# Paged attention after three conditional layers: a batch's fourth value gather is issued behind a GpSimd copy of a number that VectorE makes

## The chip, the cores and the metric

The kernel runs on one core of a Trainium2 chip, in fp32. The metric is the time of one execution in microseconds (us) of the device. The core's engines are TensorE (PE in the profile; its weight loads are PEld), VectorE (DVE), ScalarE (ACT), GpSimd (POOL) and SyncE (SP). Each engine works through its own queue of instructions in order and waits on semaphores that other engines or finished DMAs raise.

## The reference

Four residual layers on `x` of 32 batches x 32 positions x 512 channels. The first three are matrix products whose weights are picked by batch; the change does not touch them. The fourth is attention with a paged cache, and its inner part is what the change lies in:

```python
x = x + token_mixing(x); x = x + lora_linear(x); x = x + adapter_linear(x)
q = rope(rmsnorm(x @ Wq.T)); k = rope(rmsnorm(x @ Wk.T)); v = x @ Wv.T    # 32 query heads, 8 key heads, d = 128
kc = k_cache[block_table]                   # 16 pages of 32 positions: 512 cached keys a batch
vc = v_cache[block_table]                   # and 512 cached values
k_all = concat([kc, k]); v_all = concat([vc, v])                           # 544 positions
scores = where(valid, q @ k_all.T / sqrt(d), -1e30)                        # valid: cached position < cache_seqlens
x = x + (softmax(scores) @ v_all) @ Wo.T
```

## The kernel before, in words

The span has four parts: the three linear layers (to about 180 us), the projections to queries, keys and values (to about 375 us), the attention loop (to about 1086 us) and an end in which the last output projections are left over. The change lies in the attention loop alone.

**Units.** The loop runs over units (b, g): 32 batches b, and in each batch 8 key heads g, so 256 units, with a tail of 8 more steps. A unit has 128 rows: 4 query heads that share a key head, times 32 positions. Step n = 8b + g of the loop does the following, for several units at once. The order of the instructions on every engine is the order in which the program writes them (`manual_schedule`); semaphores are set by what tiles are read and written.

1. DMAs are issued: on SP's queue the key pages, queries and new values of the coming batch, and on GpSimd's queue, for batches from 2 on, one of the four gathers of cached values of the batch (`load_value_chunk`, L252: an indirect DMA of 128 rows of the cache, each row 8 heads x 128 numbers, into the tile `vt`). Gather c is issued at the step of g = c, for c = 0 to 3. The gathers of batches 0 and 1 are issued before the loop. The two batches in flight have a home pool each.
2. `scores(b, g)`: TensorE makes 288 and then 256 scores a row (L1023, L1024) in one PSUM tile `s_ps`, which has a single buffer. VectorE then does one `tensor_tensor_reduce` (L1032): it scales the scores, masks them, writes the result `pr` to SBUF, and the row's minimum to the tile `low` of 128 x 1, which has four buffers. The scores of the next unit can be written to `s_ps` only when this has read them.
3. `exponentials(b, g)`: ScalarE takes the exponential of `pr` with `low` as its bias and sums the row (L1048).
4. `flip_kept` (L1160): an earlier batch's outputs are transposed by VectorE for the output projection.
5. `place(b, q, j)` for the quad (four units) that ended before: VectorE transposes a quarter of the quad's exponentials in blocks of 32 x 32 (L1061, into `turned`, two buffers); four copies bring it into `placed`, which are shared out by a pattern: in the steps of the second quad's place two by ScalarE (L1075) and two by VectorE (L1079), in the last of these three and one, and in those of the first quad two each by ScalarE and GpSimd (L1077), or one and three in the first batches. For quad q = 0 of batch b this runs at the steps g = 4 to 7 of batch b, for q = 1 at the steps g = 0 to 3 of batch b + 1. At j = 0 GpSimd copies the columns of the new keys to `pq` (L1086), and at j = 2 TensorE transposes them (L1090, into `pn_ps`).
6. `share`: 0, 1 or 2 matmuls of the output projection (L1180, into `f_ps`) of four batches that are done. Their numbers follow a pattern of 32 steps, so four batches in a row differ and the fifth is like the first.
7. `values` for the unit 8 steps back: one product for each of the four gathers of that batch, `placed` with `vt` (L1103, into `o_ps`); with the fourth unit the new values (L1123) and the division by the sums on VectorE (L1137, L1139).

The gather and the loop's order around it read:

```python
                if g < L // P and b >= 2:
                    load_value_chunk(b, g)
                ...
                scored = scores(b, g)
                exponentials(*scored)
```

with L // P = 4. What `scores` returns ends with the tile `low` of its unit.

Of the kernel before, what the change touches and what calls it, by code (L numbers as in the profile page):

```python
# [12 lines left out]
F32 = mybir.dt.float32  # L13
# [7 lines left out]
P = 128  # L21
# [4 lines left out]
L = NPP * PSIZE  # L26
# [33 lines left out]
def cond_resid_kernel(  # L60
# [18 lines left out]
    nc = tc.nc  # L79
    H2 = D // 2  # L80

    const = ctx.enter_context(tc.tile_pool(name="const", bufs=1))
# [86 lines left out]
    def load_table(b: int):  # L169

        pages_of[b] = const.tile([1, NPP], I32, tag="pages", name=f"pages_{b}", bufs=4)
        at = B + b * NPP
        nc.sync.dma_start(out=pages_of[b], in_=pick[:, at : at + NPP])
# [34 lines left out]
    def load_keys(b: int):  # L208

        pool = homes[b % 2]  # L210
        kt = pool.tile([P, NPP + 1, HK * PSIZE], F32, tag="kt", name=f"kt_{b}")
        kts[b] = kt
# [9 lines left out]
    def load_new_keys(b: int):  # L222
        nc.sync.dma_start(out=kts[b][:, NPP, :], in_=k_d[b])

    def load_queries(b: int, q: int):

        qts[b, q] = qp.tile([P, HALF * S], F32, tag="qt", name=f"qt_{b}_{q}")
        nc.sync.dma_start(
            out=qts[b, q], in_=q_d[b][:, q * HALF * S : (q + 1) * HALF * S]
        )  # L230

    def load_inverses(b: int):
        rqs[b] = const.tile([P, 2, QUAD], F32, tag="rq", name=f"rq_{b}", bufs=2)
        nc.sync.dma_start(out=rqs[b], in_=r_d[:, b * S : (b + 1) * S])

    def page_keys(b: int):
        return [kts[b][:, n, :] for n in range(NPP)]
# [10 lines left out]
    def load_value_chunk(b: int, c: int):  # L248
        if c == 0:
            vts[b] = homes[b % 2].tile([P, L // P, HK * D], F32, tag="vt", name=f"vt_{b}")  # L250
        at = b * (L // P) + c
        nc.gpsimd.indirect_dma_start(  # L252
            out=vts[b][:, c, :],
            out_offset=None,
            in_=v_cache,
            in_offset=bass.IndirectOffsetOnAxis(ap=v_idx[:, at : at + 1], axis=0),
        )

    def load_new_values(b: int):

        vn = vnp.tile([P, HK // QUAD, D], F32, tag="vn", name=f"vn_{b}")
        vns[b] = vn
        for u in range(QUAD):
            nc.sync.dma_start(
                out=vn[u * S : (u + 1) * S, :, :],
                in_=v_d[b * S : (b + 1) * S, :].rearrange("s (q u d) -> u s q d", u=QUAD, d=D)[u],
            )
# [57 lines left out]
    def store_values(vs, c: int, t: int, eng):  # L325
        c0 = (c - (HQ + HK) // REP) * HID
        eng.dma_start(out=v_d[t * P : (t + 1) * P, c0 : c0 + HID], in_=vs)
# [589 lines left out]
    def load_wo(h: int):  # L917
        i, h0 = (0, h) if h < HQ - LATE else (1, h - (HQ - LATE))
        nc.sync.dma_start(out=wos[i][:, h0 : h0 + 2, :], in_=o_d[:, h : h + 2, :])
# [93 lines left out]
    def quad_of(b: int, g: int):  # L1013
        return b, g // QUAD

    def scores(b: int, g: int):
        kt, qt = kts[b], qts[quad_of(b, g)]
        kt4 = kt.rearrange("d n (h o) -> d n h o", h=HK)

        ps = ps_s.tile([P, 2 * L], F32, tag="s", name=f"s_ps_{b}_{g}")  # L1020
        u = g % QUAD
        q = qt[:, u * REP * S : (u + 1) * REP * S]
        nc.tensor.matmul(ps[:, first:L], q, kt4[:, :N_LOW, g, :], start=True, stop=True)  # L1023
        nc.tensor.matmul(  # L1024
            ps[:, L : first + LT], q, kt4[:, N_LOW:, g, :], start=True, stop=True
        )
        if u == 0:
            prs[quad_of(b, g)] = tp.tile([P, QUAD, LT], F32, tag="pr", name=f"pr_{b}_{g}")
        pr = prs[quad_of(b, g)][:, u, :]
        low = tp.tile([P, 1], F32, tag="low", name=f"low_{b}_{g}", bufs=4)  # L1030

        nc.vector.tensor_tensor_reduce(  # L1032
            pr,
            ps[:, first : first + LT],
            mask,
            rqs[b][:, g // QUAD, u : u + 1],
            3.0e38,
            ALU.add,
            ALU.min,
            low,  # L1040
        )
        return b, g, pr, low

    def exponentials(b: int, g: int, pr, low):
        quad, u = quad_of(b, g), g % QUAD
        if u == 0:
            dens[quad] = tp.tile([P, QUAD], F32, tag="den", name=f"den_{b}_{g}", bufs=4)
        nc.scalar.activation(  # L1048
            pr, pr, AF.Exp, bias=low, scale=-1.0, accum_out=dens[quad][:, u : u + 1]
        )  # L1050
# [99 lines left out]
    def flip_kept(n: int):  # L1150

        while kept and kept[0][3] <= n:
            b, q, o, _ = kept.pop(0)
            t, j = divmod(b, BT)
            if (t, q) not in ots:
                i = (2 * t + q) % 3
                ots[t, q] = places[i].tile(
                    [P, HALF, P], F32, tag=f"ot_{i}", name=f"ot_{t}_{q}", bufs=1
                )
            nc.vector.transpose(  # L1160
                ots[t, q][:, :, j * S : (j + 1) * S],
                o.rearrange("p (k d) -> p k d", d=S),
            )
# [3 lines left out]
    def load_residual(t: int):  # L1167
        x3s[t] = tp.tile([P, HID], F32, tag="os", name=f"x3_{t}")
        nc.sync.dma_start(out=x3s[t], in_=x_d[t])
# [83 lines left out]
    with tc.manual_schedule(engines=order):  # L1253
        for n in range(N + LAG):
            b, g = divmod(n, HK)
            if n == FILLED + 2:
                pa.close()
                late = ctx.enter_context(tc.tile_pool(name="b_w", bufs=1))
                places.append(late)
                wos[1] = late.tile([P, LATE, HID], F32, name="wo_1")  # L1260
            if BEGIN <= n <= N and n % (BT * HK) == 0:

                load_residual((n - BEGIN) // (BT * HK))
            if n < N:
                if g == 0 and b >= 1:
                    load_queries(b, 1)
                if g == 0 and 1 <= b < B - 1:
                    load_keys(b + 1)
                    load_new_keys(b + 1)
                    keys.dsts = page_keys(b + 1)  # L1270
                    keys.transfer(slice(0, 12))
                if g < L // P and b >= 2:
                    load_value_chunk(b, g)
                if g == QUAD and b < B - 1:
                    load_queries(b + 1, 0)
                    load_inverses(b + 1)
                    if b >= 1:
                        keys.transfer(slice(12, NPP))
                    if 1 <= b < B - 2:
                        load_table(b + 2)  # L1280
                if g == QUAD + 1 and b >= 1:
                    load_new_values(b)
                if g == QUAD + 2 and b < B - 2:
                    keys = Picked(nc.sync, k_cache, pages_of.pop(b + 2), range(NPP), K_SHAPE)
                scored = scores(b, g)
                exponentials(*scored)
            flip_kept(n)
            anew = n >= LAG and not filled
            if not anew:
                fill(n)  # L1290
            if n in unstored:
                store_values(*unstored.pop(n))
            if n == QUAD + 1:
                load_new_values(0)
            if n in WO_AT:
                load_wo(2 * WO_AT.index(n))
            if QUAD <= n < N + QUAD:
                bq, i = divmod(n - QUAD, HK)
                q, j = divmod(i, QUAD)
                if j == 0:  # L1300
                    gather_new(bq, q)
                if j == 2:
                    flip_new(bq, q)
                place(bq, q, j)
            begins = (n - BEGIN) % (BT * HK) == 0
            if not begins:
                share(n)
            if n >= LAG:
                values(*units[n - LAG])
            if anew:  # L1310
                fill(n)
            if begins:
                share(n)
            if n < N and g == HK - 1 and b < B - 1:
                see_keys(b + 1)
            if n > N + QUAD:
                at = 4 * (n - N - QUAD - 1)
                finish(NT - 1, range(at, at + 4))
        assert not dens and not prs and not pos and not placed and not pns
        load_residual(NT - 1)  # L1320
        flip_kept(N + LAG)
        finish(NT - 1, range(3 * QUAD, HALF))
        finish_by_halves(NT - 1)
# [76 lines left out]
```

## Time and profile before

| What | Value |
|---|---|
| median of 3 runs | 1136.5 us (1135.73 to 1137.75) |
| the profiled execution's own time | 1136.3 us |
| its span, first to last instruction | 1134.5 us |
| granted TensorE clock | 1.0 |
| PE busy, whole span | 1119.1 us, 99% |
| PE busy in the attention loop, 375 to 1086 us | 703.6 of 711 us |
| VectorE, ScalarE, GpSimd busy in the loop | 562.8, 539.4, 302.9 us |
| the gathers L252 on GpSimd, all | 128 times, 0.95 us each (median) |
| a gather from its issue to its landing | 4.5 / 7.7 / 9.9 us (least, median, most) |
| the reduction L1032 on VectorE | 256 times, 0.78 us each |

How to read it: the span is the time from the first to the last instruction of one profiled execution, and 1.8 us of that execution lie outside it. "Busy" is time in which the engine has an instruction under way. In the timeline a line is: start in us from the span's start, busy us, engine, source line, operation, the tile written, an arrow, and the tiles read, shapes, and how many instructions of this kind the row takes together. A square bracket at its end gives the idle time before it and what is held to have ended it.

### The profile page before, as it was taken

The numbers are of one execution on the slowest core, as the hardware profiler recorded it, in microseconds if no ns is written. First come the engines' busy times: TensorE is split into PE (matmuls) and PEld (weight loads), VectorE is DVE, ScalarE is ACT, GpSimd is POOL, SyncE is SP. The second block draws the span as 40 slices with busy tenths as digits, with TensorE's granted clock in tenths as the row PEclk, the third lists the DMA queues.
The fourth block names the chain that finished last, engine by engine and source line by source line (L and its number), as shares of the span: only waits on it lengthen the run. The fifth ranks groups of instructions, "written<-read, shape, count | busy, mean of one in ns | idle before, by whom it ended". The sixth has DMA issues, their size and how long they took to land.

```text
span 1134.5 us, 19093 instructions
## 1 busy us (share of the span) xinstructions
PE 1119.1 (99%) x5480; PEld 738.0 (65%) x5480; DVE 812.3 (72%) x1674; ACT 739.3 (65%) x1885; POOL 561.0 (49%) x730
## 2 busy tenths in 40 slices
PE   8999999999999899999999999999999999999998
PEld 5554444444444688777777777777777777777766
DVE  2510688887877578878778878887877787877861
ACT  1211377676666677678877777777777877777850
POOL 3411689899798455543444344334433443344410
PEclk9999999999999999999999999999999999999999
DMA  8998447688886687778767756775777676766600
GB/s 319 391 419 352 177 130 211 162 246 221 210 234 176 203 267 264 254 255 301 241 210 243 260 190 212 264 244 183 234 239 240 199 234 223 253 201 212 231 28 10
DMA packets 173355, 259.24 MB, mean 229 GB/s; under 512 B 31522, under 2 KB 130466, under 8 KB 168770
## 3 DMA queue, kind: packets, MB, share of 16 engines
q1 hardware_dynamic: 152226, 184.22, 51.4%
q0 software_dynamic: 20016, 71.97, 17.8%
q10 hardware_dynamic: 1008, 1.84, 0.4%
q8 instruction: 44, 0.72, 0.3%
q14 instruction: 61, 0.50, 0.1%
HBM read 228.46 MB, written 37.88 MB: 235 GB/s over the span
## 4 chain that ended last, share of the span: by engine, by line
PE 61%; DVE 2%; ACT 0%; issue 0%; DVEq 0%
PE o_ps L1103 19%; PE f_ps L1180 18%; PE s_ps L1023 11%; PE s_ps L1024 9%; PE o_ps L1123 2%; PE pn_ps L1090 1%; PE f_ps L1200 1%; PE f_ps_last L1200 1%; DVE placed L1079 1%; PE qkv L312 1%; DVE pr L1032 0%; DVE turned L1061 0%; ACT placed L1075 0%; DVE os L1139 0%; DVE ot L1160 0%
## 5 line engine op out<-in xcount | busy, mean ns | idle before, releaser
L1075 ACT COPY placed<-turned 32x512 f32<-32x512 f32 x524 | 322.6, 616 | 30.2 <-DVE turned L1061 24.2
L1103 PEld LDWEIGHTS o_ps<-vt,placed 128*128 128x128 f32 x2048 | 264.2, 191 | 110.9 <-issue 74.6
L1032 DVE CUSTOM_DVE_ANT_0 pr<-s_ps,mask,rq 128x544 f32<-128x544 f32 x256 | 200.4, 783 | 129.6 <-PE s_ps L1024 106.4
L1048 ACT ACTIVATE pr<-pr,low 128x544 f32<-128x544 f32 x256 | 191.6, 748 | 142.6 <-DVE low L1032 116.1
L1077 POOL COPY placed<-turned 32x512 f32<-32x512 f32 x279 | 169.6, 608 | 222.2 <-DVE turned L1061 173.5
L1103 PE MATMUL o_ps<-vt,placed 128*128 128x128 f32 x2048 | 272.0, 276 | 3.9 <-DVE os L1139 3.3
L1180 PE MATMUL f_ps<-wo,ot 128*128 128x512 f32 x480 | 240.6, 593 | 0.0
L1061 DVE STREAM_TRANSPOSE turned<-pr 128x512 f32<-128x512 f32 x256 | 178.6, 698 | 0.1
L1023 PE MATMUL s_ps<-kt,qt 128*128 128x288 f32 x512 | 174.0, 421 | 4.2 <-DVE low L1032 2.4
L1024 PE MATMUL s_ps<-kt,qt 128*128 128x256 f32 x512 | 152.3, 379 | 0.0
L252 POOL DMA_INDIRECT vt<-in_v_cache_dram,v_idx x128 | 124.3, 971 | 36.6 <-issue 25.7
L1024 PEld LDWEIGHTS s_ps<-kt,qt 128*128 128x128 f32 x512 | 97.3, 190 | 26.8
L438 POOL TENSOR_TENSOR ra<-ra,rs 128x512 f32<-128x512 f32 x80 | 103.8, 1303 | 10.7 <-DVE rs L433 8.1
L1079 DVE COPY placed<-turned 32x512 f32<-32x512 f32 x221 | 101.9, 461 | 5.6
L1180 PEld LDWEIGHTS f_ps<-wo,ot 128*128 128x128 f32 x480 | 86.9, 190 | 25.1 <-issue 13.9
L1086 POOL COPY pq<-pr 128x128 f32<-128x128 f32 x64 | 18.5, 288 | 151.6 <-ACT pr L1048 111.2
L1023 PEld LDWEIGHTS s_ps<-kt,qt 128*128 128x128 f32 x512 | 78.2, 191 | 17.3 <-DVE low L1032 6.1
L451 ACT ACTIVATE sq<-x 128x128 f32<-128x128 f32 x256 | 76.2, 301 | 19.8 <-DVE x L409 13.6
L548 ACT COPY r<-m 128x512 f32<-128x512 f32 x80 | 46.3, 579 | 52.4 <-PE m L393 50.4
L393 PE MATMUL m<-t_pair,x_sums 128*128 128x512 f32 x160 | 75.4, 594 | 0.7 <-ACT r L548 0.7
L393 PE MATMUL m<-w_pair,x3t 128*128 128x512 f32 x160 | 75.2, 592 | 0.0
L393 PE MATMUL m<-w_pair,x_sums 128*128 128x512 f32 x160 | 72.1, 593 | 0.0
(129 smaller groups left out, 1231.8 us busy)
## 6 DMA issues: line engine op xcount, KB each, us to landing
kt<-in_k_cache_dram SPq DMA_DIRECT2D x512, 128.0 KB
wa<-in_w_adapt_dram SPq DMA_DIRECT2D x32, 1024.0 KB
q_d<-st SPq DMA_DIRECT2D x128, 128.0 KB
qt<-q_d SPq DMA_DIRECT2D x64, 256.0 KB
w_pair<-in_w_qkv_dram SPq DMA_DIRECT2D x20, 512.0 KB
o_d<-in_w_o_dram SPq DMA_DIRECT2D x16, 512.0 KB
wo<-o_d SPq DMA_DIRECT2D x16, 512.0 KB
k_d<-st SPq DMA_DIRECT2D x32, 128.0 KB
```

Of the source, the lines that this page charges most:

```text
L252: nc.gpsimd.indirect_dma_start(out=vts[b][:, c, :], out_offset=None, in_=v_cache, in_offset=bass.IndirectOffsetOnAxis(ap=v_idx[:, at : at ...
L393: nc.tensor.matmul(ps, of[:, k], by[:, k], start=(not more and k == 0), stop=(k == KH - 1), skip_group_check=more,)
L1023: nc.tensor.matmul(ps[:, first:L], q, kt4[:, :N_LOW, g, :], start=True, stop=True)
L1024: nc.tensor.matmul(ps[:, L : first + LT], q, kt4[:, N_LOW:, g, :], start=True, stop=True)
L1032: nc.vector.tensor_tensor_reduce(pr, ps[:, first : first + LT], mask, rqs[b][:, g // QUAD, u : u + 1], 3.0e38, ALU.add, ALU.min, low,)
L1048: nc.scalar.activation(pr, pr, AF.Exp, bias=low, scale=-1.0, accum_out=dens[quad][:, u : u + 1])
L1061: nc.vector.transpose(part, pr)
L1075: nc.scalar.copy(dst, src)
L1077: nc.gpsimd.tensor_copy(dst, src)
L1079: nc.vector.tensor_copy(dst, src)
L1103: nc.tensor.matmul(po, pt[:, c, :], vt[:, c, g * D : (g + 1) * D], start=(c == 0 and q == 0), stop=(c == L // P - 1 and q == 1),)
L1180: nc.tensor.matmul(pfs[t][:, :HID], ots[t, h // HALF][:, h % HALF, :], wo(h), start=(h == 0), stop=(h == (HQ if t < NT - 1 else HALF) - 1),)
```

## The change

The fourth gather (c = 3) of batches 2 to 31 is no longer issued at the head of the step g = 3. It is issued at the step g = 2, behind the instructions of `scores`, and ahead of it GpSimd copies one number, the first row of the `low` that VectorE's reduction of unit g = 2 has just made, to a tile `seen` that nothing reads. As GpSimd's queue is in order, the gather comes behind that copy, and the copy waits for the reduction. The first three gathers stay where they are, and in the order of GpSimd's queue the fourth passes no other instruction.

```diff
     def quad_of(b: int, g: int):
         return b, g // QUAD
 
+    seen = const.tile([1, 1], F32, name="seen")
+
+    def see_reduced(low):
+        nc.gpsimd.tensor_copy(seen, low[:1, :])
+
     def scores(b: int, g: int):
 ...
-                if g < L // P and b >= 2:
+                if g < 3 and b >= 2:
                     load_value_chunk(b, g)
 ...
                 scored = scores(b, g)
+                if g == 2 and b >= 2:
+                    see_reduced(scored[-1])
+                    load_value_chunk(b, 3)
                 exponentials(*scored)
```

On the other engines' queues the instructions and their order are the same. One wait is new there: the tile `low` of unit 2 gets its buffer back with unit 6, so VectorE's reduction of unit 6 now waits for GpSimd's copy too. The instruction takes that wait itself and a separate semaphore instruction ahead of it takes the one for TensorE.

## The prediction

> **What bounds the kernel now.** I read the page, then the waits, then the timeline of single batches. From the page (head, and the first line of its chain):
>
> ```profile
> span 1134.5 us, 19093 instructions
> ...
> PE 1119.1 (99%) x5480; PEld 738.0 (65%) x5480; DVE 812.3 (72%) x1674; ACT 739.3 (65%) x1885; POOL 561.0 (49%) x730
> ...
> PEclk9999999999999999999999999999999999999999
> ...
> PE 61%; DVE 2%; ACT 0%; issue 0%; DVEq 0%
> ```
>
> TensorE is busy throughout at full clock. Freeing GpSimd, VectorE or the DMAs gains nothing by itself; what can be won or lost is the little time in which a matmul waits. I number a batch's units 0 to 7, call "step" the time from a unit's first score matmul (L1023) to the next unit's, and "reduction" L1032. The view of waits, VectorE:
>
> ```profile
> DVE pr L1032 <- PE s_ps L1024: 106.4, 110, 4.5
> ...
> DVE pr L1032 <- PE pn_ps L1090: 14.8, 24, 0.7
> ```
>
> (Columns: total us, count, longest.) The second line is odd: 24 reductions sit up to 0.7 us, put down to a small transposition that they don't read. The timeline shows where, here batch 18 from unit 2 on (start, length, engine):
>
> ```profile
> 779.43 0.94 POOL L252 DMA_INDIRECT vt<-in_v_cache_dram,v_idx  x1 [0.30 <-issue]
> 779.59 1.02 DVE L1079 COPY placed<-turned 32x512 f32<-32x512 f32 x2
> ...
> 779.83 0.59 PE L1024 MATMUL s_ps<-kt,qt 128*128 128x256 f32 x2
> ...
> 781.23 0.78 DVE L1032 CUSTOM_DVE_ANT_0 pr<-s_ps,mask,rq 128x544 f32<-128x544 f32 x1 [0.62 <-PE pn_ps L1090]
> ...
> 782.12 0.71 PE L1023 MATMUL s_ps<-kt,qt 128*128 128x288 f32 x2
> ...
> 785.60 0.75 PE L1023 MATMUL s_ps<-kt,qt 128*128 128x288 f32 x2
> ...
> 787.53 0.97 PEld L1103 LDWEIGHTS o_ps<-vt,placed 128*128 128x128 f32 x8 [0.72 <-ACT placed L1075]
> ...
> 788.52 0.65 PE L1023 MATMUL s_ps<-kt,qt 128*128 128x288 f32 x2
> ```
>
> Unit 2's scores end at 780.42, VectorE's copies at 780.61, yet the reduction starts at 781.23. I read this place in batches 2 to 31. In 24 of them (all but 2, 8, 17, 21, 22, 31) it starts 0.78 to 0.92 us after the **end of the fourth gather** (here 780.37), whether the scores ended 0.19 before that end (batches 3, 4), 0.06 after, or 0.35 after (5, 9, 13, 25, 29). The delay follows the gather, not the scores; by what mechanism the profile does not say. I call it the hold. Behind the first three gathers, each followed at once by other GpSimd work, it does not show (unit 1's reduction starts 0.27 us after the third, as soon as VectorE is free).
>
> Batch 22 tries the change out: its first gather came 2.2 us late, so the fourth began after unit 2's reduction had ended (871.98).
>
> ```profile
> 870.52 0.59 PE L1024 MATMUL s_ps<-kt,qt 128*128 128x256 f32 x2
> ...
> 871.19 0.78 DVE L1032 CUSTOM_DVE_ANT_0 pr<-s_ps,mask,rq 128x544 f32<-128x544 f32 x1
> ...
> 872.28 0.94 POOL L252 DMA_INDIRECT vt<-in_v_cache_dram,v_idx  x1 [0.30 <-issue]
> ...
> 872.64 0.85 DVE L1079 COPY placed<-turned 32x512 f32<-32x512 f32 x2
> ...
> 873.93 0.78 DVE L1032 CUSTOM_DVE_ANT_0 pr<-s_ps,mask,rq 128x544 f32<-128x544 f32 x1 [0.44 <-PE s_ps L1024]
> ```
>
> There the reduction begins 0.08 us after its scores, step 3 is 3.418 us (batch 18: 785.60 - 782.12 = 3.47) and step 4 is 2.770 (batch 18: 788.52 - 785.60 = 2.93).
>
> **The change part by part.**
>
> *The fourth gather leaves the hold's place.* On GpSimd it passes nothing: ahead of it only the copy is put in, and the copy waits for unit 2's reduction. What the hold costs TensorE differs by batch, because four batches make a period of the output projection. Batches 5, 9, ... 29 all take 23.280 us from unit 0 to the next batch's, held or not: slack covers it there. In the 18 batches 6, 7, 10, 11, 12, 14, 15, 16, 18, 19, 20, 23, 24, 26, 27, 28, 30, 31, step 3 is 3.42 to 3.52 and step 4 2.93: the late reduction makes the next scores late, then VectorE's transposition and ScalarE's last placed copy, for which the o_ps matmuls wait (the L1103 line above). Bringing each to 3.418 and 2.770 (batch 22; batch 8 has 3.418 and 2.771) saves 1.30 us over the 18 in step 3 and 18 x 0.159 = 2.86 in step 4. In batches 3 and 4, steps 2 and 3 are 3.017 + 2.662 and 3.116 + 2.661, where the unheld batch 2 has 2.354 + 2.560: 0.77 + 0.86 = 1.63. Together **-5.8 us**.
>
> *A wait at unit 6.* The tiles `low` have four buffers, so unit 6's reduction overwrites what GpSimd's copy reads of unit 2. GpSimd did so 11 us before, but the instruction order shows that this reduction now carries a second wait: one semaphore instruction that waits for TensorE, then the reduction with a wait for GpSimd. Unit 4's reduction has that form already. Batch 8, unit 4, then unit 6:
>
> ```profile
> 558.13 0.59 PE L1024 MATMUL s_ps<-kt,qt 128*128 128x256 f32 x2
> ...
> 558.88 0.78 DVE L1032 CUSTOM_DVE_ANT_0 pr<-s_ps,mask,rq 128x544 f32<-128x544 f32 x1 [0.18 <-PE s_ps L1024]
> ...
> 563.47 0.59 PE L1024 MATMUL s_ps<-kt,qt 128*128 128x256 f32 x2
> ...
> 564.11 0.78 DVE L1032 CUSTOM_DVE_ANT_0 pr<-s_ps,mask,rq 128x544 f32<-128x544 f32 x1 [1.25 <-PE s_ps L1024]
> ```
>
> With VectorE idle, unit 4 starts 147 ns after its scores' end, unit 6 only 38. So 0.109 us more (0 to 0.15 as ends; I take the same form's own row). In batches 5, 9, ... and 4, 8, ... unit 7's scores come 0.87 us after that reduction: hidden. In the 16 batches b mod 4 = 2 or 3 (steps of 1.97 us) they start 0.06 us after it, in lock step: 16 x 0.109 = **+1.74 us**.
>
> *GpSimd's copy and its wait.* Queued behind the waiting copy are the fourth gather and the copy L1086, which waits for ScalarE's exponentials 3 us later anyway. No row has a copy of one number; the nearest are a 128x1 memset (0.10 to 0.12 us) and L1086 (128x128, 0.288); I take 0.2, as nearer the middle. With 0.06 from VectorE to GpSimd and 0.16 from a GpSimd copy to a gather, the gather starts some 0.41 us after the reduction's end (0.32 to 0.51), 2 to 3 us later than before. Its landing is 7.7 us (median), and its first matmul reader comes 14 us after the issue. GpSimd's first placed copies of a batch (unit 4's step) come after the landings, now with 0.14 to 2.45 us to spare, so they may be up to 1 us late; GpSimd then works 1.26 us of a step of 2.7 and catches up: **0**. Uncovered it would be at most 1 us a batch.
>
> *The gather beside VectorE's copies.* They start 0.67 and 1.10 us after the reduction, 0.26 and 0.68 into the gather. Before, a copy L1079 that started 0.16 to 0.52 into a gather ran 0.414 to 0.419 us as always, one at 0.57 to 0.60 took 0.58 to 0.62, one at 0.69 took 0.50, one past 0.79 took 0.42. So about +0.08 a batch (0 to 0.2). Unit 3's reduction waits for TensorE 0.30 to 0.48 us in batches without the hold, which hides it: **0**. Without that cover it would be 18 x 0.08 = 1.5 us.
>
> Sum: -5.8 + 1.74 = **-4.05 us**. The profiled execution took 1136.3 (span 1134.5 and 1.8 around it), so 1132.25; the median of the runs shown, 1136.5, is 0.2 above it: **1132.5**. Ends: nothing paid at unit 6, 1130.7; unit 6 at 0.15 and a quarter of the holds left, 1134.6.
>
> **The rivals.**
>
> *The hold moves with the gather* (no change). Unit 3's scores will end about 0.6 us after the moved gather's end. If a hold until 0.78 to 0.92 follows there, that reduction starts 0.15 to 0.28 late, as it is in held batches now (0.30 after the scores instead of 0.04), and step 4 stays at 2.93. Then 2.86 us of the gain are lost: -1.2, **1135.3**. For: the hold did catch scores that ended 0.35 after the gather. Against: in batches 22 and 2 scores ended 0.68 and 0.71 after the fourth gather and were not held. These are just two, and 6 of 30 batches weren't held at all.
>
> *The gather blocks VectorE's copies.* If a running gather kept out both copies until its end (0.41 + 0.95 = 1.36 after the reduction), two of 0.42 would end at 2.20, and unit 3's reduction at 2.24 would be 0.29 later than TensorE allows (batch 22: 873.93 - 871.98 = 1.95). Price as before: **1135.3**. Against: in batch 18 the copies start 0.16 into the gather and both end 0.24 after it, where a blocked pair would need 0.84. The Trainium skill, "SBUF — State Buffer", section "Who interferes with whom", has this rule: VectorE and GpSimd share a port pair as an exclusive lock, and whichever starts first fully blocks the other. The trace agrees only for a copy that starts late in the gather, and then by 0.2 us at most.
>
> *The hold isn't the gather's* (slower). If it hung on unit 2 itself (its transposition L1090, ScalarE's exponentials or the landing of keys), moving the gather would leave it, and only costs remain: +1.74 at unit 6, and, as a held batch has no slack in step 4, the 1.5 of the slowed copies: **1139.7** (1138.2 if they are not slowed). It decides if unit 2's reduction still starts over 0.7 us after its scores with no gather ended near it. For: the profile names L1090, and no mechanism ties VectorE to an issued gather. Against: the spread of 0.54 us in the scores' ends that leaves the start fixed to the gather's, and batch 22.
>
> That the gather is not moved at all is excluded by GpSimd's order.
>
> **How the numbers follow.** Forecast 0.55, hold moves 0.20, blocked copies 0.05, hold stays 0.20. A measurement of this kernel tells about 0.2% (2.3 us) from no change; so the first is faster, the next two within it, the last slower. The forecast's own range is 1130.7 to 1134.6; the range given reaches through the next two (1135.3, with the same ends 1133.5 to 1136) to the foot of the last, 1130.6 to 1138.2, and leaves out its 1139.7.
>
> **What would show it.** Right: the waits line on L1090 falls from 14.8 us and 24 to nearly nothing; the fourth gather starts about 0.4 us after unit 2's reduction; steps 3 and 4 are 3.42 and 2.77 in the 18 batches; unit 6's reduction starts 0.15 after its scores. Wrong: unit 3's reduction 0.3 after its scores (hold moved, or copies of 0.9 us), unit 2's still 0.8 after (hold stays), or a placed copy on GpSimd that waits for a landing and reaches o_ps.

## The result and the profile after

The changed kernel takes 1133.0 us (median of 10 runs, 1132.2 to 1133.8) where the kernel before took 1136.5 beside it: a ratio of 0.9969, with a 95% interval of 0.9959 to 0.9979. The forecast was 1132.5. The profiled execution took 1132.9 us, with a span of 1131.1 and the same granted clock of 1.0. From the page of after (head, and the first line of its chain):

```profile
span 1131.1 us, 19153 instructions
...
PE 1116.1 (99%) x5480; PEld 738.4 (65%) x5480; DVE 811.9 (72%) x1674; ACT 739.5 (65%) x1885; POOL 568.7 (50%) x760
...
PE 58%; DVE 1%; ACT 0%; issue 0%; DVEq 0%
```

The 30 copies are there (POOL x760 instead of x730) and TensorE's busy time is 3.0 us shorter with the same number of matmuls, so part of the earlier waiting stood inside what counts as busy. In the changed kernel line numbers are 5 higher around the loop: scores L1028 and L1029, reduction L1037, VectorE's copies L1084, and L1019 is the copy to `seen`. The timeline of batch 18, from unit 2's second score matmul on:

```profile
777.65 0.59 PE L1029 MATMUL s_ps<-kt,qt 128*128 128x256 f32 x2
...
778.30 0.78 DVE L1037 CUSTOM_DVE_ANT_0 pr<-s_ps,mask,rq 128x544 f32<-128x544 f32 x1
...
779.16 0.18 POOL L1019 COPY seen<-low 1x1 f32<-1x1 f32 x1 [2.21 <-DVE low L1037]
...
779.50 0.96 POOL L252 DMA_INDIRECT vt<-in_v_cache_dram,v_idx  x1 [0.16 <-issue]
...
779.75 0.93 DVE L1084 COPY placed<-turned 32x512 f32<-32x512 f32 x2
...
779.94 0.65 PE L1028 MATMUL s_ps<-kt,qt 128*128 128x288 f32 x2
...
781.06 0.78 DVE L1037 CUSTOM_DVE_ANT_0 pr<-s_ps,mask,rq 128x544 f32<-128x544 f32 x1 [0.38 <-PE s_ps L1029]
...
783.36 0.75 PE L1028 MATMUL s_ps<-kt,qt 128*128 128x288 f32 x2
...
786.13 0.65 PE L1028 MATMUL s_ps<-kt,qt 128*128 128x288 f32 x2
```

Unit 2's scores end at 778.24 and its reduction starts at 778.30, 0.06 later instead of 0.80. The copy takes 0.18 us, and the gather starts 0.41 after the number is there, as estimated. VectorE's two copies beside it run 0.93 instead of 0.85, and unit 3's reduction still waits 0.38 for TensorE, so that is hidden. Step 3 is 783.36 - 779.94 = 3.42 and step 4 is 2.77.

What is lost shows at unit 6 of the same batch (its scores, its reduction and the next unit's scores):

```profile
789.28 0.59 PE L1029 MATMUL s_ps<-kt,qt 128*128 128x256 f32 x2
790.02 0.79 DVE L1037 CUSTOM_DVE_ANT_0 pr<-s_ps,mask,rq 128x544 f32<-128x544 f32 x1 [1.36 <-PE pn_ps L1095]
...
790.87 0.75 PE L1028 MATMUL s_ps<-kt,qt 128*128 128x288 f32 x2
```

The reduction starts 0.148 us after its scores instead of 0.038, and the next scores start 0.06 us behind its end, so they are later by the same amount.

### The profile page after: what moved, and what is told of

Its sections match the earlier page's. It is cut to its first block, busy times and chain, and to the rows that moved or that the text cites. A ratio compares the mean times of both kernels' runs of the same rounds, so it can differ in the third digit from the quotient of the medians.

```text
span 1131.1 us, 19153 instructions
## 1 busy us (share of the span) xinstructions
PE 1116.1 (99%) x5480; PEld 738.4 (65%) x5480; DVE 811.9 (72%) x1674; ACT 739.5 (65%) x1885; POOL 568.7 (50%) x760
## 4 chain that ended last, share of the span: by engine, by line
PE 58%; DVE 1%; ACT 0%; issue 0%; DVEq 0%
PE f_ps L1185 18%; PE o_ps L1108 18%; PE s_ps L1028 10%; PE s_ps L1029 8%; PE o_ps L1128 2%; PE f_ps L1205 1%; PE f_ps_last L1205 1%; PE pn_ps L1095 1%; DVE placed L1084 0%; DVE pr L1037 0%; DVE turned L1066 0%; ACT placed L1080 0%; ACT pr L1053 0%; DVE os L1144 0%; DVE ot L1165 0%
## 5 line engine op out<-in xcount | busy, mean ns | idle before, releaser
L1037 DVE CUSTOM_DVE_ANT_0 pr<-s_ps,mask,rq 128x544 f32<-128x544 f32 x256 | 200.5, 783 | 126.8 <-PE s_ps L1029 73.5
L1028 PE MATMUL s_ps<-kt,qt 128*128 128x288 f32 x512 | 172.7, 419 | 3.4 <-DVE low L1037 1.9
L1029 PE MATMUL s_ps<-kt,qt 128*128 128x256 f32 x512 | 152.3, 379 | 0.0
L1029 PEld LDWEIGHTS s_ps<-kt,qt 128*128 128x128 f32 x512 | 97.3, 190 | 26.8
L1084 DVE COPY placed<-turned 32x512 f32<-32x512 f32 x221 | 99.9, 452 | 5.6
L1028 PEld LDWEIGHTS s_ps<-kt,qt 128*128 128x128 f32 x512 | 78.3, 191 | 17.6 <-DVE low L1037 7.9
L503 DVE STREAM_TRANSPOSE st<-ra 128x512 f32<-128x512 f32 x80 | 56.3, 704 | 14.9 <-DMA q_d<-st 6.1
```

The lines of the kernel that those rows point to most:

```text
L1029: nc.tensor.matmul(ps[:, L : first + LT], q, kt4[:, N_LOW:, g, :], start=True, stop=True)
L1037: nc.vector.tensor_tensor_reduce(pr, ps[:, first : first + LT], mask, rqs[b][:, g // QUAD, u : u + 1], 3.0e38, ALU.add, ALU.min, low,)
```

## The experiments

The experiments ran in four groups, each on a chip of its own. The kernel before took 1131.2, 1136.4, 1135.9 and 1131.5 us there, a difference as large as the gain itself. So each ratio is given against the kernel before on the same chip. I call a chip "with hold" where the kernel before takes about 1136, and "without hold" where it takes about 1131.

**The copy alone, and what the hold belongs to.** The fourth gather goes back to its early place, the copy stands behind it:

```diff
                 if g < 3 and b >= 2:
                     load_value_chunk(b, g)
+                if g == 2 and b >= 2:
+                    load_value_chunk(b, 3)
...
                 if g == 2 and b >= 2:
                     see_reduced(scored[-1])
-                    load_value_chunk(b, 3)
```

> The copy alone: all four gathers come as early as before, and the one-number copy stands behind the fourth. The theory (the hold follows a row of gathers; what helps is that the fourth comes later): unit 2's reduction is held as before, 0.78 to 0.92 us after the fourth gather's end, nothing is gained, and the wait at unit 6 costs 16 x 0.109 = 1.74: about 1138.2 us, 0.15% above the kernel before. The rival (the copy itself, or GpSimd waiting for VectorE, takes the hold away): about 1133.

Measured: 1133.23 us, as the rival had it. But the kernel before took 1131.21 there (ratio 1.0016, 1.0007 to 1.0025), so nothing had been cured. Batch 18 in its timeline:

```profile
777.65 0.94 POOL L252 DMA_INDIRECT vt<-in_v_cache_dram,v_idx  x1 [0.30 <-issue]
777.81 1.03 DVE L1084 COPY placed<-turned 32x512 f32<-32x512 f32 x2
...
778.06 0.59 PE L1029 MATMUL s_ps<-kt,qt 128*128 128x256 f32 x2
...
778.87 0.79 DVE L1037 CUSTOM_DVE_ANT_0 pr<-s_ps,mask,rq 128x544 f32<-128x544 f32 x1
```

The gather ends at 778.59 as early as ever, and the reduction starts 0.28 after it, as soon as VectorE's copies end (778.84). No batch is held. So I ran the kernel before again for its profile, the changed kernel, and this one once more.

> The kernel before, unchanged, for its profile beside those of the last call, in which it took 1131.21 us and copy_behind, with the fourth gather as early as ever, had no hold at all. The theory now: whether there is a hold differs from chip to chip. If this execution is near 1131.2, unit 2's reduction starts 0.27 us or less after the fourth gather in all batches, as in copy_behind. If it is near 1136.5, it starts 0.78 to 0.92 after, in most. The rival (the hold went for another reason, in copy_behind for its copy): near 1131.2 and held.

Measured: 1136.71 us, a chip with hold. Of batches 2 to 31, 22 have unit 2's reduction 0.81 to 0.93 us behind the fourth gather; which batches escape is not quite the same set as in the first profile.

> The copy alone, behind all four gathers. Where the kernel before has the hold: it stays, and unit 6 adds 1.74: 1138.2 (if the copy itself cured it: 1133). Where it has none: 1131.2 + 1.7 = 1133.0, as in the last call.

Measured: 1139.67 us beside 1136.4, ratio 1.0028 (1.0017 to 1.0040); its profiled execution 1138.3. The same program as above, batch 18:

```profile
780.56 0.94 POOL L252 DMA_INDIRECT vt<-in_v_cache_dram,v_idx  x1 [0.30 <-issue]
780.72 1.02 DVE L1084 COPY placed<-turned 32x512 f32<-32x512 f32 x2
...
780.97 0.59 PE L1029 MATMUL s_ps<-kt,qt 128*128 128x256 f32 x2
...
782.38 0.79 DVE L1037 CUSTOM_DVE_ANT_0 pr<-s_ps,mask,rq 128x544 f32<-128x544 f32 x1 [0.63 <-PE pn_ps L1095]
```

The hold is back: 0.88 behind the gather's end (781.50). Two things follow. One and the same program has the hold in one place and not in the other; I put that down to the chip, though each chip was used only once, so the occasion is not told from the chip. And where the hold is, neither the copy nor its wait takes it away; the copy alone costs the wait at unit 6 (step 6 adds 2.1 us over the batches).

> The changed kernel beside the kernel before on this call's chip. Where the kernel before has the hold (1136.5): 1133.0, faster by 3.5. Where it has none (1131.2), only costs remain: 16 x 0.108 = 1.73 at unit 6, and some 0.3 of copies in batches 2, 3, 4 and 31: 1133.2, slower by 2.0 or 0.18%.

Measured: 1133.40 us beside 1136.4, ratio 0.9976 (0.9965 to 0.9986). Between the two profiles of that chip the loop's steps 2 to 4 are shorter by 1.69, 1.40 and 2.28 us and step 6 is longer by 2.11, as in the first pair. copy_behind_2, on the same chip, differs from this kernel in the gather's place alone and takes 6.3 us more. So on a chip with hold the gather's later place is what gains. The changed kernel itself was not run on a chip without hold; its cost there can only be estimated from copy_behind, which has the same wait at unit 6: 2.0 us.

**Does the hold need an idle GpSimd?** Six small copies right behind the fourth gather, in the kernel before:

```diff
+    pad_to = const.tile([P, 8], F32, name="pad_to")
+    def pad(count: int):
+        for _ in range(count):
+            nc.gpsimd.tensor_copy(pad_to, ident[:, :8])
...
                     load_value_chunk(b, g)
+                    if g == 3:
+                        pad(6)
```

> The kernel before, with six copies of 128 x 8 numbers on GpSimd right behind the fourth gather, which wait for nobody else. Where the kernel before has the hold: if it needs GpSimd to stop behind the gather, it goes, and the time is near 1131; if not, it stays, near 1136.5. Where it has none: no change, 1131.2.

Measured, on the chip with hold: 1136.07 us, ratio 0.9996 (0.9987 to 1.0005): no change. Batch 18 shows GpSimd at work and the reduction (L1038 here) late all the same, 0.94 after the gather's end at 781.19:

```profile
780.25 0.94 POOL L252 DMA_INDIRECT vt<-in_v_cache_dram,v_idx  x1 [0.30 <-issue]
780.66 0.59 PE L1030 MATMUL s_ps<-kt,qt 128*128 128x256 f32 x2
...
781.19 1.53 POOL L1020 COPY pad_to<-ident 128x8 f32<-128x8 f32 x6
...
782.13 0.78 DVE L1038 CUSTOM_DVE_ANT_0 pr<-s_ps,mask,rq 128x544 f32<-128x544 f32 x1 [0.70 <-PE pn_ps L1096]
```

**The wait at unit 6.** The change with `low` in eight buffers:

```diff
-        low = tp.tile([P, 1], F32, tag="low", name=f"low_{b}_{g}", bufs=4)
+        low = tp.tile([P, 1], F32, tag="low", name=f"low_{b}_{g}", bufs=8)
```

> The change with eight buffers of low in place of four. By the instruction order VectorE's reductions then carry no wait for GpSimd's copy. The theory: the changed kernel less 16 x 0.108 us at unit 6 (and less the 0.35 that batch 15 lost there), 1133.0 - 1.7 to 2.1: about 1131.1 us, unit 6's reduction 0.04 us after its scores. If the wait costs nothing that TensorE feels, 1133.0.

Measured, without hold: 1132.05 us, ratio 1.0005 (0.9996 to 1.0014): not to be told from the kernel before, and 1.2 below copy_behind.

> The change with eight buffers of low. Where the kernel before has the hold (1136.4, changed kernel 1133.2 on the mean of two calls): the changed kernel without the 16 x 0.108 of unit 6: 1131.5, faster than the kernel before by 0.43%. Where it has none: as in the first call, 0.05% slower than the kernel before.

Measured, with hold: 1131.28 us beside 1135.92, ratio 0.9954 (0.9940 to 0.9967). Unit 6 of batch 18 has its short start again, 0.04 us after the scores:

```profile
788.15 0.59 PE L1029 MATMUL s_ps<-kt,qt 128*128 128x256 f32 x2
788.79 0.78 DVE L1037 CUSTOM_DVE_ANT_0 pr<-s_ps,mask,rq 128x544 f32<-128x544 f32 x1 [1.25 <-PE s_ps L1029]
```

Against the profile of after, from another chip, step 6 is 2.11 us shorter over all batches, and the differences of the other steps cancel to 0.01. This version beats the kernel before where there is a hold and loses nothing measurable where there is none. The changed kernel was not run beside it; that low8 beats it too rests on these profiles.

**Other places for the row of gathers.** Of the four kernels that follow only row_of_three also met a chip with hold.

shift puts nine such copies ahead of the first gather of the kernel before (`if g == 0 and b >= 2: pad(9)`).

> The kernel before, with nine copies of 128 x 8 numbers on GpSimd ahead of a batch's first gather: no wait for VectorE is added, and the row of four gathers comes some 2 us later as a whole. The theory (the hold lies behind the row, wherever that is): it then ends between the scores of units 2 and 3 and holds nobody: the kernel before less up to 5.8 us, about 1131 us, with unit 2's reduction under 0.1 us after its scores in the batches where VectorE is free. The rival (unit 2 is late for a reason of its own, or only a wait helps): about 1136.5, unit 2's reduction still 0.8 late.

Measured, on the chip without hold: 1135.07 us, ratio 1.0036 (1.0025 to 1.0046). It says nothing of the hold, and it was slower by a cost that I had put at nothing: in batches 3 and 4 the first step grows by 2.0 and 2.3 us against copy_behind's. In the timeline, at the start of batch 4, the matmuls (L1109) wait for GpSimd's placed copies of batch 3, of which GpSimd makes three of four in these batches. The pads push the gathers back, and by the timeline these copies begin only at 452.27, after 6.75 us of waiting for a gather's landing; in copy_behind they do not wait for one:

```profile
455.53 4.01 POOL L1083 COPY placed<-turned 32x512 f32<-32x512 f32 x6
...
459.59 1.16 PE L1109 MATMUL o_ps<-vt,placed 128*128 128x128 f32 x8 [1.89 <-POOL placed L1083]
```

row_of_three is low8 with six such copies ahead of the first gather.

> As low8 (the fourth gather behind the copy, no wait at unit 6), with six copies of 128 x 8 numbers on GpSimd ahead of the first gather, so that the third gather ends about where the fourth ended before, just ahead of the end of unit 2's scores. If the hold follows the last gather of any row: unit 2's reduction is held again by 0.7 us or more, and the time is near 1136. If it takes four in a row: no hold, as low8, 1131.

Measured, without hold: 1132.91 us, ratio 1.0014 (1.0005 to 1.0023). The third gather did not end just before unit 2's scores: in 18 batches it ended 0.41 us behind them, so the pads pushed it further than I had reckoned. The next expectation has this wrong: the 1.03 us that it gives for these batches is the distance to the second gather's end. On a chip with hold the kernel could still tell something, in the six batches whose scores ended 0.47 behind the third gather:

> As low8, with GpSimd kept busy ahead of the first gather, so that the third gather, the last of a row of three, ends about a microsecond before unit 2's scores. Where the kernel before has the hold: if any row leaves one for 0.8 to 0.9 us behind its last gather, then batches 5, 9, ... 29, whose scores ended 0.47 after it in the first call, are held until 0.8, and the others, at 1.03, are not; if it takes four in a row, nobody is held. The time is as low8 plus 1 in both, for the late first gather. Where it has none: as in the first call.

Measured, with hold: 1132.81 us, ratio 0.9973 (0.9961 to 0.9985). Nobody is held behind the third gather. Batch 9, where the third gather ends at 575.10 and the scores at 575.56 (reduction L1043, scores L1035):

```profile
574.16 0.94 POOL L252 DMA_INDIRECT vt<-in_v_cache_dram,v_idx  x1 [0.31 <-issue]
...
574.97 0.59 PE L1035 MATMUL s_ps<-kt,qt 128*128 128x256 f32 x2
575.60 0.78 DVE L1043 CUSTOM_DVE_ANT_0 pr<-s_ps,mask,rq 128x544 f32<-128x544 f32 x1 [0.26 <-issue]
```

Five more batches are like it (13, 17, 21, 25, 29). Behind four in a row, in the four profiles with hold, scores that ended 0.33 to 0.36 after the last were held until 0.78 to 0.84 in 18 of 27 batches. Batch 5 tells a little more: its scores end 0.13 us before the third gather does and its reduction starts 0.04 after them, while behind four in a row batches 3 and 4, with scores about 0.2 before the gather's end, were held in all four profiles. So a row of three leaves a shorter hold or none; 0.47 is not 0.35, one batch is little, and which of the two stays open.

all_four puts all four gathers, in one row, behind the copy of low8.

> As low8, but all four gathers of a batch stand behind the copy of unit 2's minimum, in one row. Where the kernel before has the hold (near 1136.4): if it follows a row of four wherever it stands, unit 2's reduction is free (0.06 us after its scores) and unit 4's is late: the row ends some 5.1 us after unit 2's reduction, unit 4's scores end 0.2 to 0.4 us behind that, so it starts 0.8 to 0.9 after the row instead of 0.15 after its scores. If the hold belongs to unit 2, unit 2 is late as before; if to the early place in the batch, nobody is. The time: low8's 1131.4 if unit 4's slack of 0.5 us covers it and the landings come in time, up to 5 more if GpSimd's placed copies, which wait for the landings, are late by 4 us. Where it has none: nobody is held.

Measured, on a chip without hold: 1186.3 us, ratio 1.049. On the hold it says nothing. It shows the price of the cover on which the change's landing rests. The view of waits:

```profile
POOL placed L1082 <- DMA vt<-in_v_cache_dram,v_idx: 179.3, 25, 8.5
```

GpSimd's placed copies wait up to 8.5 us for the late landings, and TensorE's weight loads for them (37.1 us in 28 waits). In the changed kernel this line is 42.2 us in 10 waits (before: 8.4 in 2), the first placed copy of a batch is up to 0.79 us later than before, and no step of TensorE shows it.

keys_later issues 4 key pages at the head of a batch and 12 in the middle (`keys.transfer(slice(0, 4))` and `slice(4, NPP)`), in the kernel before.

> The kernel before, with 4 key pages issued on SP at the head of a batch and 12 in the middle, in place of 12 and 4, so that during the four gathers fewer transfers are under way and fewer land. Where the kernel before has the hold: if it is a backlog of landings that the gathers keep back, it is gone or shorter than 0.8, and the time is down to 5.8 us lower, near 1131; if the gathers make it alone, unit 2's reduction still starts 0.78 to 0.92 after the fourth and the time stays near 1136.4, or above, if the keys come too late for the next batch. Where it has none: no change, or above.

Measured, on the same chip without hold: 1132.67 us, ratio 1.0016 (1.0005 to 1.0028). No hold to take away there, so whether the keys' landings are part of it stays open.

## Why the prediction was right, point by point

**The hold's share.** In the pair of profiles that the forecast speaks of, the loop (first score of batch 2 to that of the last unit) is 3.02 us shorter; another 0.38 lie ahead of it, where nothing was changed. In the 18 batches steps 3 and 4 give 1.19 and 2.63 (put at 1.30 and 2.86): 17 of them do just what batch 22 showed, and batch 31 gains 0.10 in step 2 instead and loses 0.07 in step 4. Batch 31 should not have been among the 18: in the prediction's own list it is not held, and its step 3 is 3.52 in both profiles, so its length has another cause. Batches 3 and 4 give 1.43 in steps 2 and 3 (put at 1.63: 2.455 and 2.560, not batch 2's 2.354 and 2.560). The loop thus gave three quarters of the 4.05 us that were forecast. That the time came within 0.5 us of the forecast owes something to luck, the 0.38 ahead of the loop. And the range, 1130.6 to 1138.2, would have held no change as well (1136.5); it is the steps that bear the mechanism out, not the time.

**Unit 6.** 15 of the 16 batches pay 0.106 to 0.112, as the row of unit 4 had it. Batch 15 pays 0.46: the reduction there starts 0.50 after its scores, in both profiles of the changed kernel and both of copy_behind, and not in low8. Why there is not settled. Together 2.09, put at 1.74.

**Copies beside the gather.** The 0.08 was right, and hidden in the batches for which I said so. In batches 2, 3, 4 and 31 unit 3's scores end before the copies do, the cover is missing, and step 4 grows by 0.06 to 0.08 each, 0.27 in all: that term was left out.

**Rivals.** The hold did not move with the gather: in the 30 batches unit 3's reduction starts 0.04 after its scores in 26, with scores 0.5 to 0.6 behind the gather's end, and in the other four it follows VectorE's copies. The gather did not block the copies: in batch 18 they start 0.25 us into it and end at 780.68, where a pair kept out until its end (780.46) would end at 781.31. So the rule that the Trainium skill gives ("SBUF — State Buffer", "Who interferes with whom") for VectorE in its two-port modes, that whoever issues first has the shared ports for the whole instruction and fully blocks the other, is not what these two instructions do here; the measurement decides. Whether these copies run in such a mode no row says. And the hold was the gathers': copy_behind_2 keeps it with the early gather, the change removes it with the late one. What no rival held is that the hold isn't there on some chips. On those the forecast's mechanism has nothing to take away, and the likely sign is the other one; that the main pair met a hold, as the first profile had, was luck.

**A sign that failed.** I expected the waits line of L1090 to fall to nearly nothing. In after it reads

```profile
DVE pr L1037 <- PE pn_ps L1095: 44.4, 29, 2.2
```

and yet the hold is gone. All 29 are unit 6's waits, 0.8 to 2.2 us each, as in the line at 790.02: there too the transposition is TensorE's last event ahead of a start that a second wait delays. The label names what came last, not what is waited for; in before it hinted at a late start, and only the times beside the gathers showed the cause.

## What to carry to other kernels

Where an instruction starts late again and again, line its start up with the ends of everything near it: the one to which the distance stays fixed is the suspect, whatever the view of waits names. A reader of a rotating buffer on another engine can give the buffer's next writer a second wait, 0.11 us here in lock step with TensorE; more buffers took it away and made the better kernel (0.9954). And a gain whose cause is not understood should be measured on more than one chip: here it is 3.0 and 3.5 us in two places with hold and, estimated from copy_behind, a loss of 2 on chips without.

## What the runs showed of the hardware

**The hold is not VectorE's.** The trace also records when semaphores are raised, by engines and by finished DMAs. In the four profiles with four gathers in a row and with hold (the first profile, before_again, copy_behind_2, busy_after), batches 2 to 31, unit 2's reduction waits for the raise that follows the end of its scores. On the chips without hold that raise stands 0.014 to 0.015 us behind the scores' end. With hold, in 98 of the 120 cases it stands 0.34 to 1.26 us behind it, and VectorE starts 0.023 to 0.025 after the raise. So what is late is TensorE's raise; VectorE answers it at once.

**The records are not complete.** From 0.2 to 0.6 us behind the fourth gather's end I counted, over these 30 batches, 4, 10, 10 and 9 recorded raises in those four profiles, and 350 (copy_behind) and 287 (keys_later) on chips without hold. In the last 0.4 us of the gather itself the counts are 31 to 34 against 336 and 266. From 1.0 to 1.4 us behind its end they are nearer, 162 to 210 against 211 and 245. It does not follow that nothing is raised in the gap. One program, copy_behind, has 22,805 recorded raises in all without hold and 19,808 with it. And in 11 of the 120 cases the raise of unit 2's scores has no record at all, yet the reduction starts 0.04 to 0.24 us after them, not held. So on chips with hold many records are missing, most of all around the gathers.

The delay and the recording go together. Of the 27 batches whose scores ended 0.33 to 0.36 behind the last of four gathers, the 18 held ones have a record of a late raise, and the 9 that were on time have no record of it. So one rival is untested: that on these chips the recording itself holds the raise up. Every execution on record comes with a span and a granted clock of its own, so none is known to have been timed without being recorded, and whether an unrecorded execution has the hold stays open.

A fourth gather that stands alone has no such gap: from 0.2 to 0.6 us behind it there are 270 recorded raises in after and 248 in after_again, both with hold. Behind their third gathers there are 84 and 76, in low8, without hold, 133. In batch 4 of row_of_three_2 a reduction started 0.81 behind the fourth gather, with its raise 1.02 late; but there, as in batch 3, the fourth gather follows the third by 0.34 us, and the row is one of four again (in batch 3 the raise is 0.09 late). What differs between the chips, and why four in a row do it, no run here shows.
